# Moving four row sums one block earlier and folding the unary term on VectorE in an attention and binary-convolution kernel

## The chip, the cores and the metric

The kernel runs on one core of a Trainium2 chip. The metric is the device time of one execution in microseconds (us); the time before is a median of three runs. The profile is of one execution, and its times count from the first instruction.

## The reference, cut to what matters

The input x has 8 images of 64 channels and 64 x 64 pixels. Layer 0 is an attention over the 4096 pixels of an image. Only the lines that bear on the change:

```python
q_mean = q.mean(axis=2, keepdims=True)
k_mean = k.mean(axis=2, keepdims=True)
q = q - q_mean
k = k - k_mean
sim = softmax(einsum('bcn,bcm->bnm', q, k) / 8)
out = einsum('bnm,bcm->bcn', sim, v)
unary = softmax(einsum('bc,bcm->bm', q_mean[:, :, 0], k), axis=-1)
out_unary = einsum('bcm,bm->bc', v, unary)
out = out + out_unary[:, :, None]
return x + out.reshape(b, C, h, w)
```

So the mean of q over an image's pixels is needed before its first query can be centred, and the unary term adds one number per channel to every pixel of an image: a sum over all 4096 pixels of v times a weight. Layer 1 is three convolutions (1, 3 and 5 wide) of the sign of the result with binary weights, their sum, a gate per channel from the mean of the sum, and the product with the gate plus the input.

## The kernel before, in words

Two images with 64 channels each fill the 128 partitions; there are four such pairs. Each pair has eight query blocks of 512 pixels, so 32 blocks `g` run in one loop; a block is `qb` of pair `pr`. A block has 32 steps `j`, one for each 128 keys:

- `scores` (line 462): eight passes of TensorE into `ps`, then an exponential on ScalarE into `e` (line 477, four buffers);
- `weighted` (line 480): eight passes with the values `v` into `acc`, for the step before;
- `summed` (line 493): VectorE adds `e` to `es` (lines 498 and 500), for the denominators.

All the rest is put between these steps by hand. `plan(g)` fills a dictionary from step to functions with `put(step, f)`, and the loop calls them after the step's matmuls. Engines take their instructions in this order. At step 0 of block `g` stand the functions of the block's start: the copy of the finished `acc`, then what is needed at this block, then `mix_rows`, which lays the query projection `pq` of block `g+1` among the products of the convolutions of block `g-3`, and then the sums over partitions.

The names that the change and the argument touch:

- `mean_part(c)` (line 268): VectorE sums a quarter, 1024 columns, of the next pair's x into `xs` (line 278). Four of them are put at steps 14, 18, 22 and 26.
- `mean_scores` (line 280), at step 0 of `qb` 4: VectorE adds the four numbers to `xm` (line 283), and TensorE multiplies `xm` by a matrix into `pm` (line 285). `mean_scores_out` brings `pm` to `mx`, which the next pair's values and queries need.
- `begin`, at step 1 of `qb` 2: makes the next pair and issues its x load, four transfers on SyncE's queue (line 69). There are two x buffers.
- `values(i)` and `unary_part(i)` (lines 301 and 327), in `qb` 4 to 7 (pair 0: in its own block 0): the values `v` of four key tiles, and for the unary term VectorE's product of `v` with its weights, added to `vu` (128 partitions x 512 columns: four key tiles of 128 columns beside one another; line 343).
- `unary_sum` (line 345), at step 28 of `qb` 7 of the pair before (pair 0: step 31 of its block 0): sums of the weights, spread to 128 columns in `eub`.
- `unary_end` (line 352), at step 0 of a pair's `qb` 0 (pair 0: of its block 1): four matmuls of `vu`'s 128-column slices with a column of ones into one number per partition of `po` (line 355), and one for the denominator (line 358). A matmul on 32-bit data is two passes in the profile.
- `unary_out` (line 360): VectorE makes the unary term `ou` from `po` with a reciprocal and one more operation (lines 362 and 365).
- `gate_mean` at step 20 of `qb` 2 and `gate` at step 0 of `qb` 3, for the pair before: product `pg` (line 788), exponential, two small operations on VectorE.
- `store(i)` at steps 3, 6, ... 24 of `qb` 3, for the pair before: eight operations of VectorE on 512 columns (line 796), each with its transfer out.

The small PSUM tiles (`pm`, `po`, `pg`, `pq`, some of the products and sums) rotate over two buffers.

Of the kernel before, what the change touches and what calls it, by code (L numbers as in the profile page):

```python
# [22 lines left out]
ALU = mybir.AluOpType  # L23
# [3 lines left out]
P = 128  # L27
# [17 lines left out]
def conv_seq_kernel(ctx, tc, x, wq, wk, wv, vecs, w1, w3, w5, wtap, gw, out):  # L45
    nc = tc.nc
# [15 lines left out]
    def m_tile(name):  # L62
        return ps_m.tile([P, QB], F32, tag="m", name=name)

    def load_x(name, rows, queues=(nc.sync,)):
        xt = xp.tile([P, N], F32, tag="x", name=f"x_{name}")
        for c in range(4):
            cols = bass.ts(c, N // 4)
            queues[c % len(queues)].dma_start(out=xt[:, cols], in_=xf[rows, cols])
        return xt  # L70
# [34 lines left out]
    ones = cp.tile([P, P], F32, tag="ones", name="ones")  # L105
# [148 lines left out]
    class Pair:  # L254
# [88 lines left out]
                nc.vector.tensor_tensor(self.vu, old, t, ALU.add)  # L343

        def unary_sum(self):
            su = self.tile(sm, "su2", 0, (P, 2))
            nc.vector.tensor_reduce(su, self.eu, AX.X, ALU.add)
            self.eub = self.tile(sm, "cl", "s")[:, 0:P]
            for b in range(2):
                nc.vector.tensor_scalar(self.eub[:, img[b]], ones[:, 0:C], su[:, b : b + 1], None, ALU.mult)  # L350

        def unary_end(self):
            po = self.po = m_tile(f"po_{self.name}")
            for t in range(4):
                nc.tensor.matmul(  # L355
                    po[:, 0:1], self.vu[:, bass.ts(t, P)], ones[:, 0:1], start=(t == 0), stop=(t == 3)
                )
            nc.tensor.matmul(po[:, 1:2], self.eub, ones[:, 0:1], start=True, stop=True)

        def unary_out(self):  # L360
# [567 lines left out]
    def rows_of(pr):  # L928
        return slice(pr * P, (pr + 1) * P)

    def attend(pairs):
# [9 lines left out]
        def plan(g):  # L941
# [4 lines left out]
            def put(i, f, *a):  # L946
                at.setdefault(i, []).append((f, a))

            pr, qb = divmod(g, NQ)

            def nx():
                return pairs[pr + 1]
# [70 lines left out]
            if pr + 1 < n_pairs:  # L1023
                if qb == 2:
                    def begin():
                        pairs[pr + 1] = Pair(str(pr + 1), load_x(str(pr + 1), rows_of(pr + 1)))

                    put(1, begin)
                if qb == 3:
                    for c in range(4):  # L1030
                        put(14 + 4 * c, lambda c=c: nx().mean_part(c, quarters[c]))
                if qb >= 4:
                    for h in range(2):
                        i = 2 * (qb - 4) + h
                        put(14 + 8 * h, lambda i=i: nx().values(i))
                        put(17 + 8 * h, lambda i=i: nx().unary_part(i))
                    if qb == NQ - 1:
                        put(28, lambda: nx().unary_sum())
# [6 lines left out]
        for g in range(n_blocks):  # L1045
            pr, qb = divmod(g, NQ)
            at = plan(g)
            p = pairs[pr]
            for j in range(NK):
                new = (p, qb, j, p.scores(qb, j))  # L1050
                if pending is not None:
                    pending[0].weighted(*pending[1:])
                    pending[0].summed(*pending[1:])
                for f, a in at.pop(j, ()):
                    f(*a)
                pending = new
            assert not at, at.keys()
# [76 lines left out]
    with tc.If(n_good < P):  # L1134
        neg = fp.tile([P, QB], F32, tag="e5", name="neg")
        nc.vector.memset(neg, 0.0)
        with tc.For_i(0, n_pairs * P, P) as row:
# [10 lines left out]
            for qb in range(NQ):  # L1148
                mix((p, qb), None)
                for h in range(QB // P):  # L1150
                    part = sm.tile([P, 2, NQ], F32, tag="part", name=f"part_{qb}_{h}")
                    for kb_ in range(NQ):
                        ps = ps_s.tile([P, 2, QB], F32, tag="s", name=f"px_{qb}_{h}_{kb_}")
                        for b in range(2):
# [4 lines left out]
                                start=True,  # L1159
                                stop=True,  # L1160
# [90 lines left out]
```

## Time and profile before the change

| | |
|---|---|
| median of three runs | 1973.69 us (1970.32 to 1974.4) |
| the profiled execution | 1970.24 us, span 1968.1 us |
| TensorE busy | 1945.9 us, 99% |
| VectorE busy | 1627.1 us, 83% |
| ScalarE busy | 1262.8 us, 64% |
| `xs` sums, line 278 | 14 of 1024 columns, mean 1.214 us |
| `es` adds, line 500 | 960, mean 1.220 us |
| `vu` adds, line 343 | 28, mean 0.692 us |
| `po` matmul passes, line 355 | 32 |

A group's line in the profile has source line, engine and operation, then what it writes and reads with shapes; then the busy time or mean duration; "idle before" is the time the engine stood still just before it, with what it waited for. PEld is the load of weights into TensorE, which can lie beside a matmul. Where an instruction starts before the one ahead of it has ended, the timeline shows overlapping times; the start-to-start distance is then what the engine spends on one.

### The profile page before, as it was taken

How to read it: one execution, taken by the hardware profiler on the slowest of the kernel's cores; microseconds unless marked ns; L12 is line 12 of the kernel's file. 1: busy time of each engine (PE TensorE's matmuls, PEld its weight loads, DVE VectorE, ACT ScalarE, POOL GpSimd, SP SyncE). 2: the span in 40 equal slices, each digit the busy share in tenths (PEclk: the TensorE clock that was granted, in tenths of full speed). 3: DMA queues.
4: the chain of work that ended last, by engine and by line, in shares of the span. 5: the costliest groups of instructions: out<-in, count | busy, mean ns of one | idle time of the engine just before them, and what ended most of it. 6: DMA issues, size and time to landing. Idle time of an engine off the chain costs nothing.

```text
span 1968.1 us, 48733 instructions
## 1 busy us (share of the span) xinstructions
PE 1945.9 (99%) x21120; PEld 766.8 (39%) x21120; DVE 1627.1 (83%) x1976; ACT 1262.8 (64%) x1474; POOL 5.9 (0%) x26
## 2 busy tenths in 40 slices
PE   9999999999999999999999999999999999999997
PEld 4333343343333333343433333343343333333334
DVE  7878988888887798888788878888888888878876
ACT  5667666666666666666666665666666666666663
POOL 0000000000000000000000000000000000000000
PEclk9999999999999999999999999999999999999998
DMA  3010000000001010000002001000000000100001
GB/s 99 10 48 18 16 19 10 18 13 16 18 15 56 18 55 16 18 10 16 16 15 61 14 29 40 16 18 14 14 13 18 16 18 31 40 17 20 20 12 45
DMA packets 43373, 47.96 MB, mean 24 GB/s; under 512 B 16000, under 2 KB 32912, under 8 KB 43024
## 3 DMA queue, kind: packets, MB, share of 16 engines
q1 hardware_dynamic: 42400, 43.59, 8.4%
q8 instruction: 167, 2.74, 0.6%
q10 hardware_dynamic: 720, 1.18, 0.2%
q14 instruction: 54, 0.44, 0.1%
q0 software_dynamic: 32, 0.01, 0.0%
HBM read 14.89 MB, written 8.39 MB: 12 GB/s over the span
## 4 chain that ended last, share of the span: by engine, by line
PE 92%; DVE 5%; issue 1%; ACT 1%; DMA 0%; DVEq 0%; SPq 0%; ACTq 0%
PE ps L466 42%; PE acc L485 42%; PE z L680 4%; DVE es L500 4%; PE su L516 1%; PE pq L451 1%; PE pv L308 1%; PE z L751 1%; ACT e L477 1%; PE z_5d L680 0%; DMA x<-in_x 0%; DVE sb L796 0%; DVE sb L713 0%; PE warm L152 0%; PE po L355 0%
## 5 line engine op out<-in xcount | busy, mean ns | idle before, releaser
L477 ACT ACTIVATE e<-ps 128x1024 f32<-128x1024 f32 x1024 | 1049.8, 1025 | 619.1 <-PE ps L466 590.9
L500 DVE TENSOR_TENSOR es<-es,e 128x1024 f32<-128x1024 f32 x960 | 1171.2, 1220 | 184.4 <-ACT e L477 146.8
L466 PE MATMUL ps<-q,x 64*64 64x512 f32 x8192 | 1067.7, 591 | 0.9 <-DVE kb L162 0.9
L485 PE MATMUL acc<-e,v 64*64 64x512 f32 x8192 | 1064.2, 589 | 0.7 <-ACT e L477 0.3
L485 PEld LDWEIGHTS acc<-e,v 64*64 64x64 f32 x8192 | 309.5, 131 | 572.1 <-ACT e L477 307.0
L466 PEld LDWEIGHTS ps<-q,x 64*64 64x64 f32 x8192 | 307.8, 133 | 543.7 <-issue 287.9
L713 DVE SCALAR_TENSOR_TENSOR sb<-z,frac,sb 128x256 f32<-128x256 f32 x87 | 39.2, 478 | 62.6 <-PE z L680 62.6
L680 PE MATMUL z<-e,wt 64*64 64x256 bf16 x754 | 85.3, 272 | 0.1
L680 PE MATMUL z<-ec,wt 64*64 64x256 bf16 x754 | 85.3, 272 | 0.0
L680 PEld LDWEIGHTS <-wt 64*64 64x64 bf16 x1508 | 77.3, 106 | 1.1 <-issue 0.3
L680 PEld LDWEIGHTS <-wc 64*64 64x64 bf16 x1218 | 67.7, 107 | 3.6 <-issue 0.6
L498 DVE TENSOR_TENSOR es<-e,e 128x1024 f32<-128x1024 f32 x32 | 39.2, 1225 | 33.3 <-ACT e L477 33.3
L713 DVE SCALAR_TENSOR_TENSOR sb<-es_z,frac,sb 128x256 f32<-128x256 f32 x145 | 62.2, 480 | 0.0
L680 PE MATMUL z<-ec,wc 64*64 64x256 bf16 x464 | 62.0, 274 | 0.0
L529 DVE RECIPROCAL rc<-su 128x128 f32<-128x128 f32 x62 | 59.1, 953 | 0.0
L695 ACT ACTIVATE sb<-z_5d,shift,frac 128x256 f32<-128x256 f32 x58 | 29.6, 561 | 45.9 <-PE z_5d L680 45.9
L596 ACT ACTIVATE s<-x,vec 128x512 bf16<-128x512 f32 (+2 forms) x66 | 46.1, 702 | 5.2 <-DVE x L564 5.2
L680 PE MATMUL z<-e,wc 64*64 64x256 bf16 x319 | 45.4, 273 | 0.0
L458 DVE TENSOR_SCALAR q<-pq,mx 128x256 f32<-128x256 f32 x60 | 27.0, 480 | 16.7 <-PE pq L451 16.2
L507 ACT COPY o<-acc 128x1024 f32<-128x1024 f32 (+2 forms) x33 | 32.3, 981 | 1.2 <-PE acc L485 1.2
L409 ACT ACTIVATE ck<-rc,lim 128x256 bf16<-128x256 f32 x62 | 30.9, 498 | 0.0
L720 ACT COPY es_z<-z 128x1024 f32<-128x1024 f32 x29 | 29.3, 1012 | 0.0
(150 smaller groups left out, 698.3 us busy)
## 6 DMA issues: line engine op xcount, KB each, us to landing
r<-rc SPq DMA_DIRECT2D x248, 32.0 KB, 1.9
x<-in_x SPq DMA_DIRECT2D x15, 512.0 KB, 5.8
out<-sb SPq DMA_DIRECT2D x28, 256.0 KB, 2.1
ec<-e SPq DMA_DIRECT2D x29, 153.0 KB, 2.4
xc<-in_x SPq DMA_DIRECT2D x60, 64.0 KB, 2.4
ec<-e SPq DMA_DIRECT2D x29, 132.0 KB, 2.3
y<-y SPq DMA_DIRECT2D x30, 64.0 KB, 1.9
w_tap<-in_wtap SPq DMA_DIRECT2D x2, 560.0 KB, 9.8
```

The source lines that it names most:

```text
L409: nc.scalar.activation(junk[:, 0:w], r, AF.Sign, bias=lim[:, side : side + 1], scale=1.0 - 2.0 * side, accum_out=fit[:, side, i : i + 1],)
L466: nc.tensor.matmul(ps[img[h], b, :], self.x[img[b], bass.ds(j * P + h * H, H)], self.q[qb][img[b], :], start=True, stop=neg is None,)
L477: nc.scalar.activation(e, ps, AF.Exp, scale=1.0 / 8.0)
L485: nc.tensor.matmul(self.acc[qb][img[b], h, :], self.v[img[h], j, img[b]], e[img[h], b, :], start=(j == 0), stop=(j == NK - 1),)
L498: nc.vector.tensor_tensor(self.es[qb], self.first, e, ALU.add)
L500: nc.vector.tensor_tensor(self.es[qb], self.es[qb], e, ALU.add)
L507: nc.scalar.copy(self.acc[qb][:, :, c], acc[:, :, c])
L529: nc.vector.reciprocal(self.rc[:, c], self.sums_p[:, c])
L596: nc.scalar.activation(sy[n][0][:, rows, pad : pad + HH], self.x2[qb][:, r0 * HH : r1 * HH].rearrange("p (h w) -> p h w", w=HH), AF.Sign, ...
L680: nc.tensor.matmul(z[img[b], :].rearrange("p (h w) -> p h w", w=HH), taps[img[h], c * C : c * C + C], src[:, first : first + 3 * step + 1 ...
L695: nc.scalar.activation(sv[:, :, t, :], z.rearrange("p (j w) -> p j w", w=HH), AF.Identity, bias=shift, scale=frac[5][:, t : t + 1],)
L713: nc.vector.scalar_tensor_tensor(out, z.rearrange("p (j w) -> p j w", w=HH), by, out, ALU.mult, ALU.add)
```

## The change

The sums of the next pair's x are made in the block in which its load is issued (`qb` 2) instead of the one after (`qb` 3), for every pair but the first, whose block 2 also prepares the convolution weights. In `qb` 3 of these pairs VectorE also has the eight stores. And the four 128-column slices of `vu` are added up on VectorE, first the upper 256 columns to the lower 256, then the upper 128 of these to the lower, in `unary_sum`; then one matmul does for four.

```diff
         def unary_sum(self):
+            for w in (2 * P, P):
+                nc.vector.tensor_tensor(
+                    self.vu[:, 0:w], self.vu[:, 0:w], self.vu[:, w : 2 * w], ALU.add
+                )
             su = self.tile(sm, "su2", 0, (P, 2))
             nc.vector.tensor_reduce(su, self.eu, AX.X, ALU.add)
...
         def unary_end(self):
             po = self.po = m_tile(f"po_{self.name}")
-            for t in range(4):
-                nc.tensor.matmul(
-                    po[:, 0:1], self.vu[:, bass.ts(t, P)], ones[:, 0:1], start=(t == 0), stop=(t == 3)
-                )
+            nc.tensor.matmul(po[:, 0:1], self.vu[:, 0:P], ones[:, 0:1], start=True, stop=True)
             nc.tensor.matmul(po[:, 1:2], self.eub, ones[:, 0:1], start=True, stop=True)
...
-                if qb == 3:
+                if qb == (3 if pr == 0 else 2):
                     for c in range(4):
                         put(14 + 4 * c, lambda c=c: nx().mean_part(c, quarters[c]))
```

## The prediction

> **What bounds the kernel now.** The page comes first: the busy shares and the chain that ended last.
>
> ```profile
> PE 1945.9 (99%) x21120; PEld 766.8 (39%) x21120; DVE 1627.1 (83%) x1976; ACT 1262.8 (64%) x1474; POOL 5.9 (0%) x26
> PE 92%; DVE 5%; issue 1%; ACT 1%; DMA 0%; DVEq 0%; SPq 0%; ACTq 0%
> ```
>
> TensorE is the bound, but 5% of the chain (about 98 us) runs through VectorE. The question is where. The table of waits of the whole span, searched for TensorE waiting on VectorE, names one place (in total, times, longest):
>
> ```profile
> PEld pm L285 <- DVE xm L283: 7.9, 3, 3.5
> PE pm L285 <- DVE xm L283: 5.3, 2, 2.6
> ```
>
> `pm` is the matmul that needs the mean of the next pair's x. It stalls TensorE three times in weight loads, twice for 2.65 us in matmuls. Then the windows, one per query block, cut at the first score matmul after the block's mix of products (columns: length, busy PE, PEld, DVE, ACT, POOL, clock, DMA):
>
> ```profile
> 194.80:254.60 59.80, 59.80 (x630) 23.12 (x634) 52.61 (x64) 38.50 (x44) 0.00 (x0) 1.00 0.07 16
> 614.40:674.90 60.50, 60.04 (x633) 23.04 (x630) 48.53 (x60) 38.64 (x45) 0.00 (x0) 1.00 0.07 15
> 674.90:738.15 63.25, 60.53 (x634) 22.87 (x633) 57.55 (x72) 38.46 (x44) 0.00 (x0) 1.00 0.15 48
> 1158.50:1223.20 64.70, 61.99 (x630) 24.21 (x630) 57.57 (x72) 38.41 (x44) 0.00 (x0) 0.97 0.15 47
> 1643.60:1702.50 58.90, 58.88 (x628) 22.58 (x628) 52.93 (x65) 38.36 (x44) 0.00 (x0) 1.00 0.16 51
> ```
>
> In order: pair 0's block 3 (four sums of x, no stores); pair 1's block 2 (neither); block 3 of pairs 1 and 2 (four sums and eight stores); pair 3's block 3 (eight stores, no sums). Either load alone leaves VectorE at about 53 us and the block at 59 to 60 us; both together make 57.6 us and 63 to 65. The timelines show the end of such a block. VectorE in pair 1's block 3, then in pair 0's block 3, then in pair 3's:
>
> ```profile
> 724.27 1.21 DVE L278 TENSOR_REDUCE xs<-x 128x1 f32<-128x1024 f32 x1
> 725.40 7.86 DVE L500 TENSOR_TENSOR es<-es,e 128x1024 f32<-128x1024 f32 x6
> 733.18 0.15 DVE L283 TENSOR_REDUCE xm<-xs 128x1 f32<-128x4 f32 x1
> ...
> 240.76 3.88 DVE L500 TENSOR_TENSOR es<-es,e 128x1024 f32<-128x1024 f32 x3
> 245.01 1.23 DVE L500 TENSOR_TENSOR es<-es,e 128x1024 f32<-128x1024 f32 x1 [0.37 <-ACT e L477]
> ...
> 1695.48 1.22 DVE L500 TENSOR_TENSOR es<-es,e 128x1024 f32<-128x1024 f32 x1 [0.19 <-ACT e L477]
> ```
>
> An `es` add waiting for ScalarE (the bracket) means that VectorE has caught up. In pair 0 this happens three adds before the block's end, in pair 3 two. In pair 1 never: six adds run back to back, and `xm` is behind them. On TensorE:
>
> ```profile
> 733.38 0.38 PE L285 MATMUL pm<-xm,mm 128*128 128x1 f32 x2 [2.65 <-DVE xm L283]
> ```
>
> For the second edit, the chain around the start of pair 1:
>
> ```profile
> 489.85 0.86 PE acc L485 x8
> 490.70 0.98 PE po L355 x8
> 491.69 0.22 PE po L358 x2
> 491.91 0.82 PE pq L451 x5
> ```
>
> No gap lies between these: the unary matmuls are wholly on the bound.
>
> [...]after the gap of 2.65 us that ends at 1216.94 the granted clock is 0.50 from 1218 to 1220; after the equal gap before 733.38 it stays 1.00. [...]The `po` matmul has one moving column, and eight passes take 0.98 us, 122 ns each[...]. The `vu` adds of 512 columns took 691 to 694 ns[...].
>
> **Part by part.** *(a) The sums leave block 3 of pairs 1 and 2.* Four reduces of 1.21 us, each delaying the next instruction by 1.13, are 4.5 us less, so VectorE falls to about 53 us as in pair 3's block 3, which shows two waiting adds at its end. `xm` and `pm` stay at the start of block 4; pair 0's block 3 shows the price of that with VectorE caught up: 59.79 us from first score to first score (194.80 to 254.59, in the chain) against 58.96 for pair 3's. So both blocks should come to 59.79:
> pair 1: 738.15 - 674.93 = 63.22, less 59.79 = 3.43 us;
> pair 2: 1223.22 - 1158.50 = 64.72, less 59.79 = 4.93 us (1.5 more, from the half clock).
> Sum 8.36 us.
>
> *(b) The sums enter block 2 of pairs 1 and 2.* VectorE goes from 48.5 to about 53 us. Pair 0's block 3 ran this very mix of instructions, with the sums at the same steps, and TensorE was busy 59.80 of 59.80. Block 2 has `gate_mean` (0.155 us) besides, so the caught-up wait of 0.37 shrinks to some 0.25 and two steady ones follow. The product `pg` of the gate at the next block's start finds VectorE as now. The added wait: the first sum waits for the x load, and the `es` adds queue behind it, then ScalarE's four `e` buffers, then TensorE. But the queue runs ahead: pair 2's x was issued from 590.26, in 5.4 us each, and the transfers had ended by 599. The first sum would run near 639 (pair 0's, at 219.53, shifted by 419.62). A slack of 40 us: cost nothing. Pair 0 keeps its place, so nothing changes there.
>
> *(c) `po` loses three of four matmuls,* 6 of 8 passes: 6 x 0.1225 = 0.73 us per pair on TensorE with no gap. The following `pq` waits for `ou`, which VectorE makes after `po`, so the chain moves up as a whole.
>
> *(d) VectorE gets two adds per pair.* The trace has none of this size[...]. Lower bound: both overlap their neighbours by 0.08 (as the mixed groups do), 0.55 us; upper: the second waits 0.1 for the first (as `es` after `es`, 1.33 apart for 1.22), 0.73. I take 0.73. Queued behind: the sums of `eu`, two small scalings, `es`. In pairs 1 to 3 this is step 28 of block 7; the add after it at 485.82 waits 0.49 today, the next two also 0.49, so the delay is gone before step 31, and 3 x 0.73 = 2.2 us is gained. In pair 0 it is step 31 of block 0: the last `es` ends at about 75.9 instead of 75.2, and the reciprocal of `po`, which would start near 75.55, starts there: 0.4 us gained instead of 0.73. Sum of (c) and (d): 2.6 us.
>
> Total: 8.36 + 2.6 = 11.0 us. From the median of 1973.69: 1962.7.
>
> **Rivals.** *R1, the adds take back what `po` gives.* For it: they stand near the block's end. Against: three waiting adds follow. Time: only (a), 1973.7 - 8.4 = 1965.3.
> *R2, the stall moves.* Block 2 does not catch up, and `pg` waits there as `pm` did, by some 3.4 us at both boundaries. For it: VectorE has a reserve of only three steps. Against: pair 0's block 3. Time: 1973.7 - 11.0 + 6.9 = 1969.6.
> *R3, slower.* Block 2 has no slack at all, so that the 4.5 us end up before `pg`, each time followed by the 1.5 us of half clock, and block 3, with eight stores, starts late and keeps its own 3.4; the adds cost at four starts what `po` saves. Change: 2 x (4.5 + 1.5) = 12 lost, against 1.5 (the half clock of pair 2) gained: 1984. Milder, with half of it, 1978. For it: only that VectorE is the second bound. Against: the 12 us of its idle time in block 2 today.
>
> **How the numbers follow.** Chances: forecast 0.74, R1 0.12, R2 0.09, R3 0.05. The predicted time is the forecast's. Low end: the three times before spread from 1970.3 to 1974.4, so a median near the lowest gives 1959.3, and a second half-clock stall in the timed runs would add 1.5 to the gain: 1957.8, say 1958. High end: R1 and half of R2's stall, 1968. Faster by over 0.2% means under 1969.7: forecast, R1 and half of R2, 0.90; within, 0.06; slower, 0.04.
>
> **What would show it.** In the profile after: no matmul `pm` waiting over 1 us for `xm`; block 3 of pairs 1 and 2 near 59.8 us with VectorE near 53, block 2 still 60.5 with an `es` add waiting for ScalarE near its end; `po` at 8 passes in place of 32 for line 355, starts of pairs 0.7 us shorter; granted clock 1.00 near 1218. Wrong if block 2 grows, if `pg` or `po` waits for VectorE, or if a sum waits for the load.

## The result and the profile after

The median of four runs is 1959.57 us (1959.19 to 1959.95), against 1974.05 us (1970.32 to 1975.08, four runs) for the kernel before: a ratio of 0.993, 95% interval 0.9913 to 0.9947. The forecast was 1962.7, range 1958 to 1968. The span of the profiled execution fell from 1968.1 to 1957.0 us, by 11.1; the forecast's sum was 11.0. The medians fell by 14.5, so 3.4 us of the gain are not in the two profiles. Where these come from is the main question of the experiments. Below, a stall is a standstill of TensorE, and half clock a stretch in which the granted clock is 0.50.

The page, busy shares and chain:

```profile
PE 1941.5 (99%) x21096; PEld 763.7 (39%) x21096; DVE 1629.2 (83%) x1984; ACT 1261.7 (64%) x1474; POOL 5.9 (0%) x26
PE 97%; ACT 1%; DVE 1%; DMA 0%; issue 0%; SPq 0%; ACTq 0%; DVEq 0%
```

VectorE's work has grown, from 1627.1 to 1629.2 us, and its share of the chain has fallen from 5% to 1%: nearly the same work stands where nobody waits for it. The fall in share is not the gain: 4% of the span are about 80 us, and 11 were saved. Before, the chain ran along VectorE for most of block 3 of pairs 1 and 2; now TensorE is busy through all 59.80 us of it. The table of waits has one line left in which `pm` waits for `xm`, three weight loads with 0.8 us at most, each of which lies beside running matmuls:

```profile
PEld pm L285 <- DVE xm L283: 2.4, 3, 0.8
```

The windows of the block before pair 1, then blocks 2 and 3 of pair 1 and block 3 of pair 2 (columns as before):

```profile
434.20:495.40 61.20, 61.20 (x696) 24.29 (x696) 52.18 (x68) 40.31 (x52) 0.00 (x0) 1.00 0.07 15
613.30:673.80 60.50, 60.04 (x633) 23.05 (x630) 52.67 (x64) 38.62 (x45) 0.00 (x0) 1.00 0.07 15
673.80:733.60 59.80, 59.80 (x634) 23.13 (x630) 53.28 (x69) 38.43 (x44) 0.00 (x0) 1.00 0.16 50
1153.30:1213.10 59.80, 59.80 (x632) 23.14 (x633) 53.27 (x68) 38.44 (x44) 0.00 (x0) 1.00 0.16 50
```

VectorE's 57.6 us of block 3 have become 53.3, block 2's 48.5 have become 52.7, and block 2 is as long as it was. The timeline of VectorE at the end of block 2 and of block 3 of pair 1:

```profile
665.26 1.23 DVE L501 TENSOR_TENSOR es<-es,e 128x1024 f32<-128x1024 f32 x1 [0.39 <-ACT e L478]
666.98 1.23 DVE L501 TENSOR_TENSOR es<-es,e 128x1024 f32<-128x1024 f32 x1 [0.49 <-ACT e L478]
669.76 0.15 DVE L792 TENSOR_SCALAR gt<-gt 128x1 f32<-128x1 f32 x1 [1.56 <-ACT gt L791]
...
725.78 1.23 DVE L501 TENSOR_TENSOR es<-es,e 128x1024 f32<-128x1024 f32 x1 [0.20 <-ACT e L478]
727.49 1.23 DVE L501 TENSOR_TENSOR es<-es,e 128x1024 f32<-128x1024 f32 x1 [0.49 <-ACT e L478]
728.63 0.15 DVE L283 TENSOR_REDUCE xm<-xs 128x1 f32<-128x4 f32 x1
```

In both blocks VectorE has caught up two adds before the end, and `xm` follows an add that was not late. In block 2 it then waits 1.56 us more, for the gate's exponential (`gt`).

The chain at the start of pair 1, where the prediction shows `po` with eight passes and 0.98 us:

```profile
490.30 0.31 PE po L358 x2
490.62 0.22 PE po L359 x2
```

A table of block lengths in us from the chain of waits, from the first score matmul after a block's mix to the next such:

| block | before | after |
|---|---|---|
| last before pairs 1, 2, 3 | 61.92, 61.91, 61.92 | 61.24, 61.25, 61.24 |
| block 2 of pairs 1, 2, 3 | 60.51, 60.52, 60.52 | 60.51, 60.51, 60.51 |
| block 3 of pairs 1, 2, 3 | 63.22, 64.72, 58.96 | 59.79, 59.79, 58.96 |
| the rest of pairs 1 and 2, per block | 58.96 or 60.0 | 58.96 or 60.0 |

### The profile page after: what moved, and what is told of

The parts are those of the page before. It is cut to its first block, busy times and chain, and to the rows that moved or that the text cites. A ratio compares the mean times of both kernels' runs of the same rounds, so it can differ in the third digit from the quotient of the medians.

```text
span 1957.0 us, 48693 instructions
## 1 busy us (share of the span) xinstructions
PE 1941.5 (99%) x21096; PEld 763.7 (39%) x21096; DVE 1629.2 (83%) x1984; ACT 1261.7 (64%) x1474; POOL 5.9 (0%) x26
## 4 chain that ended last, share of the span: by engine, by line
PE 97%; ACT 1%; DVE 1%; DMA 0%; issue 0%; SPq 0%; ACTq 0%; DVEq 0%
PE ps L467 45%; PE acc L486 44%; PE z L681 4%; PE su L517 1%; PE pq L452 1%; PE pv L308 1%; PE z L752 1%; ACT e L478 0%; PE z_5d L681 0%; DMA x<-in_x 0%; DVE es L501 0%; PE warm L152 0%; PE pre L1095 0%; DVE r L554 0%; ACT o L508 0%
## 5 line engine op out<-in xcount | busy, mean ns | idle before, releaser
L478 ACT ACTIVATE e<-ps 128x1024 f32<-128x1024 f32 x1024 | 1049.1, 1024 | 618.0 <-PE ps L467 599.0
```

The lines of the kernel that those rows point to most:

```text
L478: nc.scalar.activation(e, ps, AF.Exp, scale=1.0 / 8.0)
```

## The experiments

Eight kernels ran, four to a chip. On the first chip the kernel before has a median of 1972.64 us over 42 runs (1970.43 to 1977.95), on the second 1973.31 over nine (1970.25 to 1974.93). The ratios are to the kernel before on the same chip. All block lengths are from first score to first score.

**Only the sums moved,** in the kernel before.

```diff
-                if qb == 3:
+                if qb == (3 if pr == 0 else 2):
                     for c in range(4):
```

> Only the sums of x moved (pairs 1 and 2, one block earlier); the unary term as before. Theory (the two parts are independent; the sums give 3.43 + 4.93 us of span): block 3 of pairs 1 and 2 is 59.8 us from first score to first score, span 1968.1 - 8.4 = 1959.7, no pm wait over 1 us, starts of pairs 1 to 3 still 61.9. If the half clock after the stalls is what spreads the times of the kernel before, the timed runs lie within 1 us of each other, near 1962. Rival (the stall moves to the gate's product pg): block 2 grows from 60.5 by 1 us or more and the span is above 1963.

Measured: median 1962.60 us (1962.48 to 1963.81), ratio 0.9949 (0.9936 to 0.9963). Blocks 3 of pairs 1 and 2 take 59.79 and 59.80, blocks 2 stay at 60.5, and the starts of the pairs at 61.9. The timed runs lie within 1.3 us, a little more than expected. The span of the profiled execution, 1961.7, is 2 us over the expected one; block 1 of pair 0 took 59.06 instead of 57.45 there, and its clock shows why (windows):

```profile
78.40:90.00 11.60, 11.60 (x100) 3.83 (x100) 6.46 (x6) 5.36 (x6) 0.00 (x0) 0.86 0.04 11
```

Mean clock 0.86 over 11.6 us, in a stretch that the change does not touch; the other four executions have spans of 1960.4 to 1961.6. Finer windows show half clock for 3.4 us, and TensorE at work in the 3.4 us before it:

```profile
74.90:78.30 3.40, 3.37 (x34) 1.74 (x26) 1.96 (x5) 2.30 (x6) 0.00 (x0) 1.00 0.02 5
78.30:81.70 3.40, 3.40 (x20) 1.03 (x20) 0.17 (x2) 1.02 (x1) 0.00 (x0) 0.50 0.13 39
```

So half clock can come without a stall as well. Ahead of it lie the ten passes of `po`, each with one moving column; the kernel before has the same passes there at a clock of 1.00, so what set it off stays open. The stall did not move to the gate, and the median gained 10.0 us, of which the stalls and one half clock (8.4) leave 1.6 unexplained.

**Only the unary fold:** the changed kernel with the sums put back.

```diff
-                if qb == (3 if pr == 0 else 2):
+                if qb == 3:
                     for c in range(4):
```

> Only the unary term folded on VectorE; the sums of x stay in block 3. Theory: each start of pairs 1 to 3 is 0.7 us shorter (61.2), that of pair 0's block 1 some 0.5, span about 2.4 us less where the half clock falls the same way; both stalls of 2.65 us before pm stay, and the timed runs scatter by 3 us or more as those of the kernel before do. Rival (the adds take it back): no change of the starts, a wait of the po matmul or of the last es add at step 31 in its place.

Measured: median 1969.60 us over 14 runs (1967.69 to 1973.3), ratio 0.9983 (0.9975 to 0.9991). The starts of pairs 1 to 3 take 61.25, and the spread remains, 5.6 us. This time the half clock followed the stall of pair 1, whose block took 66.11, and pair 2's took 63.19. The waits and the windows after the two stalls:

```profile
PE pm L285 <- DVE xm L283: 5.3, 2, 2.6
```

```profile
735.00:741.00 6.00, 6.00 (x109) 5.25 (x100) 1.27 (x3) 1.69 (x3) 0.00 (x0) 0.58 0.09 25
1218.00:1224.00 6.00, 4.84 (x118) 3.90 (x122) 2.81 (x8) 1.79 (x3) 0.00 (x0) 1.00 0.09 25
```

Equal stalls, unequal ends: 2.9 us lost to the clock in pair 1 (66.11 less 63.22), nothing in pair 2. In the profile of the kernel before it was the other way round, with 1.5. The fold alone gives 3.0 us of median; the sum of the two parts is 13.1, against 14.5 for both in the first comparison and 13.5 on the second chip, each median of before being uncertain by its spread. So the parts add up within what the medians of before differ by.

**The stall filled with idle work,** in the kernel before.

```diff
             self.pm = m_tile(f"pm_{self.name}")
+            if self.name in ("2", "3"):
+                for _ in range(9):
+                    nc.tensor.matmul(self.pm[:, P : 2 * P], ones, ones, start=True, stop=True)
             nc.tensor.matmul(self.pm[:, 0:1], mm, xm, start=True, stop=True)
```

> The kernel before, with nine matmuls of ones by ones (128 columns, into columns of pm that nothing reads) put in front of the pm matmul of pairs 2 and 3, so that TensorE works while it would stand still for 2.65 us. Theory (the idle gap brings the half clock, and this spreads the times): the granted clock is 1.00 through both starts of block 4, both blocks 3 are about 63.2 us, span near 1966.6, and all timed runs lie within 1 us of each other, below the median of the kernel before by some 5 us. Rival (the clock and the spread have another cause): the same spread of 4 us and the same median as before.

Measured: median 1969.54 us over 21 runs (1969.0 to 1971.75), ratio 0.9982 (0.9975 to 0.9988). TensorE's timeline at the stall of pair 1:

```profile
731.54 2.27 PE L287 MATMUL pm<-ones 128*128 128x128 f32 x18
734.26 0.38 PE L288 MATMUL pm<-xm,mm 128*128 128x1 f32 x2 [0.44 <-DVE xm L283]
```

The gap has shrunk from 2.65 to 0.44 us while `xm` comes as late as ever: the blocks take 63.30 and 63.29, with a granted clock of 1.00 in both. No useful work was saved, and yet the median is 3.1 us lower (5 expected) and the spread 2.8 us instead of 7.5 (1 expected). The mean granted clock of each execution is on record: it is 0.997 or 0.998 in all 21 here, and 0.996 or less in 38 of the 42 of the kernel before. Their means, 0.9972 and 0.9954, differ by an estimated 3.5 us of full clock over the span of 1968 us. So at these two places it is the gap that brings the half clock, and the half clock makes up most of the spread. What the remaining 2.8 us are is not shown; a half clock without a stall, as above, or a later start could be among them: in the profiles of this document, that of the last kernel apart, block 1 of pair 0 starts between 77.7 and 80.2 us. The account of the sums closes within the uncertainty of the medians: two blocks shorter by 3.43 us are 6.9, the clock 3.1, together 10.0, which is what the move alone gave.

**The sums earlier in the same block,** in the kernel before.

```diff
-                        put(14 + 4 * c, lambda c=c: nx().mean_part(c, quarters[c]))
+                        put((14 if pr == 0 else 2) + 4 * c, lambda c=c: nx().mean_part(c, quarters[c]))
```

> The kernel before, with the four sums of pairs 1 and 2 left in block 3 but put at steps 2, 6, 10 and 14 instead of 14, 18, 22 and 26. Theory (VectorE's total in the block is the limit: 57.6 us of work in 59.8): the work is the same, the block stays at 62.5 to 63.2 us; what is not waited for before pm is lost within the block, as ScalarE and TensorE wait for the four e buffers. Rival (only the late position of the sums matters): VectorE has caught up by the block's end, the pm wait is 0.8 us and the block 59.8, a gain near the 8.4 us of the move to block 2.

Measured: median 1970.79 us over 13 runs (1969.8 to 1975.83), ratio 0.9994 (0.9986 to 1.0003): no difference from before. The blocks take 63.60 and 63.59, slightly more than the 62.5 to 63.2 expected. The waits of pair 1's block 3:

```profile
PEld acc L485 <- ACT e L477: 15.5, 31, 1.7
ACT e L477 <- DVE es L500: 8.9, 11, 1.5
PE pm L285 <- DVE xm L283: 1.0, 1, 1.0
```

The line of ScalarE in the same block of the kernel before:

```profile
ACT e L477 <- DVE es L500: 5.6, 7, 1.3
```

The wait before `pm` is 1.0 us in place of 2.65, and what left it came back as ScalarE waiting for `es` (8.9 us against 5.6) and TensorE for `e`. Not the position of the sums but VectorE's total in the block sets its length. That the median is no worse although the blocks are longer fits the clock: the gap is 1.0 us, the granted clock of the profile is 1.00 in both blocks, and the mean clock of the 13 executions is 0.996 to 0.998.

**How much block 2 can take.** The changed kernel with some sums made twice in block 2 of pairs 1 and 2; with `c >= 2` two more, with `c >= 0` four more:

```diff
                         put(14 + 4 * c, lambda c=c: nx().mean_part(c, quarters[c]))
+                        if pr >= 1 and c >= 2:
+                            put(14 + 4 * c, lambda c=c: nx().mean_part(c, quarters[c]))
```

> The changed kernel with the sums of the third and fourth quarter made twice in block 2 of pairs 1 and 2 (the second writes the same numbers), 2.3 us more work of VectorE in that block. Theory (the reserve of block 2 is the two waits for ScalarE at its end, 0.39 and 0.49, and the 1.56 us for which VectorE waits for the gate's exponential, 2.4 us in all): the block stays at 60.5 to 60.7, span within 0.5 us of the changed kernel. Rival (block 2 is full as it is): each block 2 grows by 2 us or more, span above 1960.

> The same with all four sums made twice, 4.5 us more. Theory (reserve 2.4 us): block 2 of pairs 1 and 2 grows by some 2.1 us each, to 62.6, and VectorE has no waiting es add before its end; span near 1961. Rival (VectorE is hidden whatever it does): no change. Rival (block 2 is full as it is): growth by 4.5 us each, span 1966.

For comparison, the changed kernel itself on the second chip, where these two and the next experiment ran:

> The changed kernel, unaltered, on the chip of the next three, for comparison with them. Span 1957.0 to 1957.7, no granted clock under 1.00 at the starts of block 4, timed runs within 1 us of each other near 1959.6.

Measured: unaltered, median 1959.86 us (1958.84 to 1961.76; the profiled execution, the slowest, came to block 1 of pair 0 2.5 us later than the one shown above, so its span of 1959.6 missed the 1957.0 to 1957.7 expected: TensorE waits 1.9 us for x near its start, and half clock follows from 8.25 to 11.65 us; the 36 passes of `warm` from 8.79 take 5.59 us instead of 4.21), ratio 0.9929 (0.9916 to 0.9943). Two more sums: 1959.57 us, blocks 2 at 60.51: free. Four more: 1963.67 us (1963.21 to 1963.83), blocks 2 at 62.49 and 62.48. The timeline of VectorE at the end of that block:

```profile
662.91 2.47 DVE L278 TENSOR_REDUCE xs<-x 128x1 f32<-128x1024 f32 x2
665.30 7.86 DVE L501 TENSOR_TENSOR es<-es,e 128x1024 f32<-128x1024 f32 x6
673.08 0.15 DVE L792 TENSOR_SCALAR gt<-gt 128x1 f32<-128x1 f32 x1
```

No add waits any more, and the gate's addition follows the last `es` at once, without its former wait of 1.56 us. The reserve read from three waits (0.39, 0.49 and 1.56, in all 2.4 us) held to 0.1 us: 4.5 less 2.4 is 2.1, measured 1.97. In this block VectorE is hidden up to that sum and costs in full beyond it; 2.3 us of added work lay under it, 4.5 over it.

**The small products off the block's start.** The changed kernel, with other places for what the start waits for; `mean_sum` is the part of `mean_scores` that makes `xm`:

```diff
-            if qb == 3 and pr >= 1:
-                put(0, pairs[pr - 1].gate)
+            if qb == 2 and pr >= 1:
+                put(30, pairs[pr - 1].gate)
+            if qb == 3 and pr + 1 < n_pairs:
+                put(28, lambda: nx().mean_sum())
+                put(30, lambda: nx().mean_scores())
+                put(31, lambda: nx().mean_scores_out())
             if qb == 4 and pr + 1 < n_pairs:
-                put(0, lambda: nx().mean_scores())
-                put(0, lambda: nx().mean_scores_out())
                 put(1, lambda: nx().value_weights())
-            if qb == 0 and pr >= 1 or g == 1:
-                put(0, pairs[g // NQ].unary_end)
-                put(0, pairs[g // NQ].unary_out)
+            if g == 1:
+                put(9, pairs[0].unary_end)
+                put(10, pairs[0].unary_out)
+            if qb == NQ - 1 and pr + 1 < n_pairs:
+                put(31, lambda: nx().unary_end())
+                put(31, lambda: nx().unary_out())
```

> The changed kernel with the three small products taken off the block's start, where pq waits for what VectorE or ScalarE makes of them: xm at step 28 and pm at step 30 of block 3, the gate at step 30 of block 2, po and ou at step 31 of block 7 (pair 0: at steps 9 and 10 of its block 1). Theory (at a start the round trip is waited for, in the steps it lies beside the score matmuls; the passes themselves stay on TensorE): block 3 goes from 59.8 to 59.3, block 2 from 60.5 to 59.3, the starts of pairs 1 to 3 from 61.24 to 60.5, that of pair 0 by 0.5, three times each but the last: 7.9 us, span near 1949.1. Rival (in the steps the round trip is waited for just the same[...]): span above 1955.

Measured: median 1953.50 us (1953.07 to 1957.52), ratio to the kernel before 0.9905 (0.989 to 0.992), 6.4 us under the changed kernel on the same chip; span 1951.2. Block 2 takes 59.43 where it took 60.51, block 3 59.43 where it took 59.79, the last block before a pair 60.69 where it took 61.24; pair 0 gained nothing to speak of (its block 1 grew from 57.44 to 58.14, having begun 0.6 earlier). Sum: 3 x (1.08 + 0.36 + 0.55) = 6.0 of the 7.9 us expected. The chain at the gate's new place and at the start after it:

```profile
664.17 0.31 PE pg L790 x2
664.48 1.02 PE ps L468 x8
665.50 0.86 PE acc L487 x8
...
668.08 0.43 PE pq L453 x8
```

`pg` costs its 0.31 us and 0.16 more on the score group after it (1.02 for 0.86); `pq` goes through at once. The expectation had left out the 0.16. Several things move in this kernel, but each falls in another block, so the block lengths tell them apart. This version beats both kernels.

## Why the prediction was right

- *VectorE overfull in block 3 of pairs 1 and 2.* Shown: block lengths 59.79 as forecast, and the sums placed earlier in the same block did not shorten it. The two gains, 3.43 and 4.93, came to the hundredth. That the whole span agrees with the forecast to 0.1 us is in part luck: the blocks that the change touches and the start of pair 0 give 8.36 + 2.02 + 0.38 = 10.8, and the other 0.3 us lie behind the last block's start, where no edit stands.
- *Block 2 takes the sums for nothing.* Shown, by its unchanged 60.5 us and by the two doublings. The reasoning was a little off: of three waiting adds forecast two are left, and the larger part of the reserve, the 1.56 us of waiting for the gate's exponential, had not been counted. R2 and R3 would have needed block 2 to grow with the four sums that the change puts there.
- *The x load is early enough.* Right: in the profile after, the four sums of pair 1's block 2 start at 638.43, 645.48, 652.29 and 658.53 and wait for nothing.
- *`po` gives 0.73 us at three starts.* Measured 0.68, 0.66 and 0.68. The forecast took the mean of eight passes. The first two take 0.31 us and each two behind them 0.22, as the chain after the change shows: three times 0.22 went, 0.66. The records of these weight loads are 0.19 us each (line 355 before, mean 191 ns); how much of a pass is loading, the runs do not show. Pair 0: 0.4 forecast; block 1 begins 0.38 earlier although its scores began 0.24 later, so 0.6. Its chain does go through VectorE's adds and `ou`, as foreseen; of the 0.2 us more, about 0.14 come from the adds, which cost less than forecast (below), and from the reciprocal, which starts 0.08 before the last `es` ends (76.00 against 74.86 + 1.22).
- *The two new adds, 0.73 us.* Measured 0.66 from the start of the first to the start of what follows (483.13 to 483.79), which is what the 0.73 stood for, and 0.74 or 0.75 to the end of the second; the durations are 421 and 292 ns. The bounds of 0.55 and 0.73 were the author's estimate. From the adds of the kernel before (512 columns in 692 ns, 1024 in 1220) a straight line gives an estimate of 428 and 296 ns, and with the overlap of 0.08 and the wait of 0.1 bounds of 0.56 and 0.74. R1 did not come: the adds at steps 30 and 31 wait for ScalarE again.
- *What was mis-sized: the half clock.* The forecast took 1.5 us for it, the one event in the profile, and subtracted the span's gain from a median. The median of before contains more: in other executions the clock drops after the other stall, or for longer (2.9 us in the fold-only kernel). The prediction had a second such drop only in the low end of its range. The filled stall puts the loss near 3.1 us at the median, 1.6 more than forecast. That is about half of the 3.1 us between 1962.7 and the measured 1959.57; about 1 us more is the median that it started from, 1973.69 of three runs, where 42 runs gave 1972.64. The rest is not told apart from the spread of the medians of before, which on three occasions were 1974.05, 1972.64 and 1973.31.
- *The high end of the range.* R1 and half of R2's stall come to 1965.3 + 3.4 = 1968.7 us, not 1968; nothing hangs on it.

## What to carry to other kernels

Where a bound engine waits in few blocks, lay the blocks' windows side by side and look for one that has each load alone: pair 0 and pair 3 priced this change before it was made. The reserve of a hidden engine in a block can be read as the sum of its waits between the added work and the point where somebody needs it, waits for a round trip included: here 2.4 us, and 2.3 us of added work were free. A value that makes a round trip through another engine is worth trying some steps before the start that needs it; here it cost there its own passes (0.31 us) and 0.16 us more, except in pair 0, where nothing was gained.

## What the runs showed of the hardware

A standstill of TensorE of 2.65 us is followed by half clock in some cases and not in others: after pair 2's stall but not pair 1's in the profile before, the other way round in the fold-only kernel, at stalls of the same length. It cost nothing, 1.5 or 2.9 us. The half clock lasts 3.4 us in the first case (1217.4 to 1220.8) and 6.8 in the second (733.3 to 740.1). It also followed a standstill of 1.9 us at the start of the unaltered kernel on the second chip, and none at all in block 1 of pair 0 when only the sums were moved, 3.4 us in each case. What decides it is not shown.

In the profile before, VectorE kept to the order of the program at the end of pair 1's block 3: the last sum that `xm` reads had ended at 725.48 us, and `xm` started at 733.18, behind the six adds put ahead of it.

In 42 executions of the kernel before, the time goes with the mean granted clock: the four at 0.997 have a median of 1971.1 us, the seven at 0.994 one of 1975.1. Filling the gap with eighteen useless passes made the kernel 3.1 us faster at the median, with the blocks as long as before. A single profile shows one draw of this, so a difference of medians can be larger than the difference of two profiles.
